# A graph-attention kernel on one core: ScalarE's part of the row loop traced one or two tiles later, counts and casts moved from VectorE to ScalarE

## The chip, the core and the metric

The kernel runs on one core of one Trainium2 chip. The metric is the device time of one execution in microseconds (us); lower is better. TensorE does the matrix products, VectorE, ScalarE and GpSimd do elementwise work, and SyncE issues most of the loads. Each engine runs its own instructions in order and waits for the others by semaphores. In the lines of the profile TensorE is PE (its weight loads PEld), VectorE DVE, ScalarE ACT, GpSimd POOL, SyncE SP.

## The reference

x has 3327 rows of 1024 numbers, adj is a symmetric 0/1 matrix of 3327 x 3327 with the diagonal set and about 17 ones in a row, and the weights are 1024 x 1024.

```python
h = maximum(layernorm(x), 0)
f = h @ Wf + bf
g = h @ Wg + bg
e = relu(f @ g.T)
scores = where(adj > 0, e, -9e15)
out = x + softmax(scores, axis=1) @ (h @ W + bW)
```

## The kernel before

The adjacency is sparse, so the kernel (`edge_path`) works on lists of neighbours. It has two parts. A dense fallback (`dense_path`) would run only if a list had not held its row's neighbours; with these inputs it does not.

**The first part** loops over 26 tiles `t` of 128 rows of x and adj (the last has 127). For each tile:

- `degrees(t)` loads the adjacency rows into `r`, of which there are four buffers. ScalarE turns them into floats in place with a Relu and sums them into the row's degree `deg` (L435). GpSimd multiplies by 1 + the column number (L436), so that `r` holds the numbers of the neighbours and zeros. The last two tiles do this in two halves.
- `normed(t)` makes h. It loads the rows of x into `xt` and finds mean and deviation: on VectorE for odd tiles (`bn_stats`, `bn_aggr` into `mv`, L406, L408; then ScalarE takes `nmr` and `rstd` from `mv`, L409, L410), on ScalarE for even ones (sum L414, L415, Square L417, Sqrt L418). VectorE takes the reciprocal (L419), ScalarE scales `nmr` (L420), computes the Relu of the normalized rows (L421) and issues the store to the table `hd` in memory (L423).
- `edges(t, r)` is VectorE's: in each of 16 segments of the row the 8 largest numbers (L446), 128 candidates `cand`; the count of positive ones (`cnt`, L448); then five times the 8 largest of the candidates into `lst` with a match_replace that takes these out (L452, L454), which gives the list of up to 40 neighbours; limits (L455), the cast into the payload `pay` (L456), the degree limited and cast (`dg`, L458, L459), and a one-hot of the degree `oh` (L460).
- `counted(t - 4)` counts, on TensorE with the result in `pre`, how many rows of each degree have come (L467, L472), and VectorE picks each row's rank out of it (`hit`, L469).
- `store_lists` writes the payload of four tiles to the table `pd`.

Beside this the loop prepares A = Wf Wg^T: in the first 8 tiles TensorE transposes row blocks of Wg, which ScalarE copies to `WgT` (L489, L490); in the next 8 iterations `make_A(c)` transposes a row block of Wf, multiplies (`ps_A`, L519, and `ps_u`, L525), and ScalarE copies the result (L522, L526). `make_rows` makes three rows from the biases (casts `terms`, L541).

After the loop VectorE and TensorE sort the rows by degree into `perm` (L575 to L612). `bads` collects what would call for the fallback.

**The second part** takes 128 rows at a time in the order of `perm`, gathers their lists and the h rows of their neighbours, and computes scores, softmax and output (L638 to L775). It takes most of the time and is not edited.

The order of instructions on each engine is set by a scheduler: it follows the order in which the program is traced as a priority and lets later instructions pass where it expects a wait. Each engine then runs its list strictly as compiled. A buffer is free again when the last reader of the tile before has finished.

Of the kernel before, what the change touches and what calls it, by code (L numbers as in the profile page):

```python
# [8 lines left out]
FP = mybir.dt.float32  # L9
I32 = mybir.dt.int32  # L10
AF = mybir.ActivationFunctionType
ALU = mybir.AluOpType
AX = mybir.AxisListType
# [6 lines left out]
BF = mybir.dt.bfloat16  # L20
SEG = 16
KM = 40
NBIN = 64
# [266 lines left out]
def edge_path(ctx: ExitStack, tc: tile.TileContext, x, adj, Wf, bf, Wg, bg, W, bW, out, flag):  # L290
# [10 lines left out]
    nc = tc.nc  # L301
    N, D = x.shape
    O = W.shape[1]
    P = 128
# [4 lines left out]
    NT = (N + P - 1) // P  # L309
# [4 lines left out]
    def rows(t):  # L314
        return min(P, N - t * P)
# [7 lines left out]
    const = ctx.enter_context(tc.tile_pool(name="const", bufs=1))  # L323
# [7 lines left out]
    eps = const.tile([P, 1], FP, name="eps")  # L331
# [2 lines left out]
    nc.gpsimd.iota(iotak, pattern=[[1, KM]], base=0, channel_multiplier=0, allow_small_or_imprecise_dtypes=True)  # L334
    ones3 = const.tile([3, P], BF, name="ones3")
    nc.gpsimd.memset(ones3, 1.0)
    bads = const.tile([P, NT + 2], FP, name="bads")
    nc.gpsimd.memset(bads, 0.0)


# [1 line left out]
    perm = const.tile([P, NT], I32, name="perm")  # L342
# [8 lines left out]
    with ExitStack() as part1:  # L351
        pool1 = lambda name, bufs, **kw: part1.enter_context(tc.tile_pool(name=name, bufs=bufs, **kw))
        c1 = pool1("c1", 1)
        wrow = pool1("wrow", 3)
        wT = pool1("wT", 2)
        ln = pool1("ln", 5)
        lnj = pool1("lnj", 1)
        kpool = pool1("key", 4)
        cpool = pool1("cand", 2)
        p_tr = pool1("p_tr", 2, space=PSUM)  # L360
        p_mm = pool1("p_mm", 2, space=PSUM)
        p_u = pool1("p_u", 1, space=PSUM)
# [29 lines left out]
        nc.gpsimd.memset(oh[:, NT - 1, :], 0.0)  # L392
        pre = p_c.tile([P, NBIN], FP, name="pre")

        def normed(t):

            n = rows(t)
            xt = ln.tile([P, D], FP, name="xt")
            for a, m in pieces(t):
                nc.sync.dma_start(xt[a : a + m], x[t * P + a : t * P + a + m, :])  # L400
            rstd = ln.tile([P, 1], FP, name="rstd")
            nmr = ln.tile([P, 1], FP, name="nmr")
            if t % 2:
                st = ln.tile([P, D // CB, 6], FP, name="st")
                for c in range(D // CB):
                    nc.vector.bn_stats(st[:n, c, :], xt[:n, c * CB : (c + 1) * CB])  # L406
                mv = ln.tile([P, 2], FP, name="mv")
                nc.vector.bn_aggr(mv[:n], st[:n])  # L408
                nc.scalar.activation(nmr[:n], mv[:n, 0:1], AF.Copy, scale=-1.0)  # L409
                nc.scalar.activation(rstd[:n], mv[:n, 1:2], AF.Sqrt, bias=eps[:n])  # L410
            else:
                sums = ln.tile([P, 2], FP, name="sums")
                j = lnj.tile([P, D], BF, name="lnj")
                nc.scalar.activation(j[:n], xt[:n], AF.Copy, accum_out=sums[:n, 0:1])  # L414
                nc.scalar.activation(nmr[:n], sums[:n, 0:1], AF.Copy, scale=-1.0 / D)  # L415
                j = lnj.tile([P, D], BF, name="lnj")
                nc.scalar.activation(j[:n], xt[:n], AF.Square, bias=nmr[:n], accum_out=sums[:n, 1:2])  # L417
                nc.scalar.activation(rstd[:n], sums[:n, 1:2], AF.Sqrt, bias=eps[:n], scale=1.0 / D)  # L418
            nc.vector.reciprocal(rstd[:n], rstd[:n])  # L419
            nc.scalar.activation(nmr[:n], nmr[:n], AF.Copy, scale=rstd[:n])  # L420
            nc.scalar.activation(xt[:n], xt[:n], AF.Relu, bias=nmr[:n], scale=rstd[:n])  # L421
            for a, m in pieces(t):
                nc.scalar.dma_start(hd[t * P + a : t * P + a + m, :], xt[a : a + m])  # L423

        def degrees(t):
            n = rows(t)
            r = kpool.tile([P, N], FP, name="r")
            a = r.bitcast(I32)
            for b, m in pieces(t):
                nc.sync.dma_start(a[b : b + m], adj[t * P + b : t * P + b + m, :])  # L430

            cuts = [0, SEG // 2 * SW, N] if t >= NT - 2 else [0, N]
            for i, (b, e) in enumerate(zip(cuts, cuts[1:])):
                to = deg[:n, t : t + 1] if not i else half[:n]
                nc.scalar.activation(r[:n, b:e], a[:n, b:e], AF.Relu, accum_out=to)  # L435
                nc.gpsimd.tensor_mul(r[:n, b:e], r[:n, b:e], iotaj[:n, b:e])  # L436
                if i:
                    nc.scalar.activation(deg[:n, t : t + 1], deg[:n, t : t + 1], AF.Identity, bias=half[:n])
            return r

        def edges(t, r):

            n = rows(t)
            cand = cpool.tile([P, SEG * 8], FP, name="cand")
            for s in range(SEG):
                nc.vector.max(cand[:n, s * 8 : s * 8 + 8], r[:n, s * SW : min(N, (s + 1) * SW)])  # L446
            pos = cpool.tile([P, SEG * 8], BF, name="pos")
            nc.vector.tensor_scalar(  # L448
                pos[:n], cand[:n], 0.0, None, op0=ALU.is_gt, op1=ALU.add, accum_out=cnt[:n, t : t + 1]
            )  # L450
            for i in range(0, KM, 8):
                nc.vector.max(lst[:n, i : i + 8], cand[:n])  # L452
                if i + 8 < KM:
                    nc.vector.match_replace(cand[:n], lst[:n, i : i + 8], cand[:n], 0.0)  # L454
            nc.vector.tensor_scalar(lst[:n], lst[:n], float(N), 1.0, op0=ALU.min, op1=ALU.max)  # L455
            nc.vector.tensor_scalar(pay[:n, t, :KM], lst[:n], -1.0, None, op0=ALU.add)  # L456
            dg = cpool.tile([P, 1], FP, name="dg")
            nc.vector.tensor_scalar(dg[:n], deg[:n, t : t + 1], float(NBIN - 1), None, op0=ALU.min)  # L458
            nc.vector.tensor_copy(pay[:n, t, KM : KM + 1], dg[:n])  # L459
            nc.vector.tensor_scalar(oh[:n, t, :], iotad[:n], dg[:n], None, op0=ALU.is_equal)  # L460

        def counted(t):

            n = rows(t)


            nc.tensor.matmul(pre, tri, oh[:, t, :], start=(t == 0), stop=False, skip_group_check=True)  # L467
            hit = cpool.tile([P, NBIN], FP, name="hit")
            nc.vector.scalar_tensor_tensor(  # L469
                hit[:n], pre[:n], 1.0, oh[:n, t, :], op0=ALU.mult, op1=ALU.mult, accum_out=rp[:n, t : t + 1]  # L470
            )
            nc.tensor.matmul(pre, low, oh[:, t, :], start=False, stop=(t == NT - 1), skip_group_check=True)  # L472
# [60 lines left out]
        def make_rows():  # L533

            ps = p_u.tile([P, P], FP, name="ps_u")
            for k in range(KD):
                nc.tensor.matmul(ps[0:1, 0:1], bfT[:, k : k + 1], bgT[:, k : k + 1], start=(k == 0), stop=(k == KD - 1))
            nc.scalar.copy(cols[:, :KD], v_ps)
            nc.scalar.copy(cols[0:1, 2 * KD :], ps[0:1, 0:1])
            for i in range(3):  # L540
                nc.vector.tensor_copy(terms[:, i, :], cols)  # L541
                if i < 2:
                    nc.vector.tensor_sub(cols, cols, terms[:, i, :])
            for row, first in ((v3, 0), (bW3, KD)):
                for o in range(OH):
                    ps = p_mm.tile([P, CB], FP, name="ps_A")
                    for k in range(CB // P):
                        c = first + o * (CB // P) + k
                        nc.tensor.matmul(ps[:3, k * P : (k + 1) * P], terms[:, :, c], identb, start=True, stop=True)
                    nc.scalar.copy(row[:, o * CB : (o + 1) * CB], ps[:3])  # L550
            ps = p_u.tile([P, P], FP, name="ps_u")
            nc.tensor.matmul(ps[:3, 0:1], terms[:, :, 2 * KD], identb[:, 0:1], start=True, stop=True)
            nc.scalar.copy(v3[:, D : D + 1], ps[:3, 0:1])

        for t in range(NT):
            r = degrees(t)
            normed(t)
            edges(t, r)
            if t >= LAG:
                counted(t - LAG)  # L560
            if t % 4 == 3 and t > 4:
                store_lists(t - 7, t - 3)
            if t < KD:
                load_Wg(t)
            elif t < 2 * KD:
                make_A(t - KD)
            if t == 2 * KD:
                make_rows()
        for t in range(NT - LAG, NT):
            counted(t)  # L570
        store_lists(20, NT)
# [34 lines left out]
            )  # L606
        tens = c1.tile([P, NT], FP, name="tens")
        nc.vector.tensor_copy(tens, ps[:, NT : 2 * NT])
        nc.vector.scalar_tensor_tensor(perm, ps[:, :NT], float(P), tens, op0=ALU.mult, op1=ALU.add)
        over = c1.tile([P, 1], FP, name="over")  # L610
        nc.vector.tensor_scalar(over, part, float(rows(NT - 1)), float(N), op0=ALU.is_ge, op1=ALU.mult)
        nc.vector.tensor_tensor(final, perm[:, NT - 1 : NT], over, op=ALU.add)  # L612
# [2 lines left out]
        nc.vector.tensor_reduce(bads[:, NT : NT + 1], ne, AX.X, ALU.max)  # L615
        nc.vector.tensor_scalar(ne, deg, 1.0, None, op0=ALU.is_lt)
        nc.vector.tensor_reduce(bads[:, NT + 1 : NT + 2], ne, AX.X, ALU.max)


    W_sb = ctx.enter_context(tc.tile_pool(name="W", bufs=1)).tile([P, KD, O], FP, name="W_sb")  # L620
# [239 lines left out]
```

## Time and profile before

| | us |
|---|---|
| median of 14 runs | 1463.4 |
| lowest and highest of them | 1441.2, 1489.4 |
| profiled execution, own time | 1469.4 |
| its span, first to last instruction | 1467.7 |
| tile loop of the first part, until the last multiply on GpSimd ends | 263.7 |
| `perm` ready, second part begins | 284 |

| Engine | busy in the whole span | share |
|---|---|---|
| VectorE | 1221.4 us | 83% |
| TensorE | 1179.9 us | 80% |
| GpSimd | 875.0 us | 60% |
| ScalarE | 474.7 us | 32% |

The shares are means over two parts with different limits: ScalarE, with 32% over the whole, is busy for 69% of the time from tile 2 to tile 24 in the first part. So what an edit of the first part is worth must be read from that stretch alone. A line of the timeline has its start, its duration, the engine, the line of the kernel, the operation, result and inputs with their shapes, and in brackets how long the engine had been idle and what ended that. A line of the list of waits has who waited for whom, then the total, the number of waits and the longest.

### The profile page before, as it was taken

To read this page: it belongs to the slowest core of one execution; us is meant where nothing else is said; L and a number is where in the kernel's file an instruction comes from. 1 tells how busy PE (TensorE), PEld (TensorE's weight loads), DVE (VectorE), ACT (ScalarE), POOL (GpSimd) and SP (SyncE) were. 2 spreads that over 40 slices of the span, in tenths; PEclk is the share of its full clock that TensorE was granted. 3 is DMA by queue.
4 is the path that set the end of the run, shared out by engine and by line. 5 is a ranking of instruction groups with operands and counts; after the bars stand their busy time and mean duration, and the time that the engine had idled before them with its cause. 6 is when DMAs were issued, how large, how long until landed. Compare 5 with 4: busy or idle time off the path is not lost.

```text
span 1467.7 us, 14137 instructions
## 1 busy us (share of the span) xinstructions
PE 1179.9 (80%) x4355; PEld 685.5 (47%) x4355; DVE 1221.4 (83%) x2550; ACT 474.7 (32%) x738; POOL 875.0 (60%) x628
## 2 busy tenths in 40 slices
PE   4579996057188798999779878899889998999784
PEld 4445453034065455555345444555445554555331
DVE  4888889609979889898887789898899989999980
ACT  6666767101063144433122321222222222121110
POOL 8677776262656466666464456666667676666501
PEclk9999998579599899999889888999999999999887
DMA  9897895392678798887695677777878878788812
GB/s 369 334 346 315 309 324 170 113 407 65 235 243 294 243 329 281 306 284 229 241 320 171 232 262 268 260 231 245 263 245 290 281 234 257 259 274 276 256 30 59
DMA packets 97710, 372.52 MB, mean 254 GB/s; under 512 B 14268, under 2 KB 14684, under 8 KB 94297
## 3 DMA queue, kind: packets, MB, share of 16 engines
q0 software_dynamic: 79552, 286.85, 58.3%
q1 hardware_dynamic: 10860, 70.49, 12.5%
q10 hardware_dynamic: 7212, 14.18, 2.8%
q8 instruction: 36, 0.59, 0.2%
q14 instruction: 50, 0.41, 0.1%
HBM read 343.67 MB, written 27.80 MB: 253 GB/s over the span
## 4 chain that ended last, share of the span: by engine, by line
PE 27%; issue 26%; POOL 17%; DVE 15%; DMA 5%; ACT 5%; another core or an unknown queue 4%; POOLq 0%; ACTq 0%; SPq 0%; DVEq 0%
PE ps_o L759 13%; POOL r L436 9%; PE ps_q L667 8%; DVE y L747 6%; POOL G L638 6%; DMA G<-hd,pi 4%; PE yT_ps L725 3%; DVE junk L684 3%; DVE cand L446 2%; ACT G L741 2%; PE ps_A L519 1%; DMA res<-in_x_dram,perm 1%; POOL res L638 1%; DVE sc L684 1%
## 5 line engine op out<-in xcount | busy, mean ns | idle before, releaser
L638 POOL DMA_INDIRECT G<-hd,pi x468 | 545.4, 1165 | 276.5 <-issue 111.3
L684 DVE CUSTOM_DVE_ANT_0 junk<-G,q 128x1024 bf16<-128x1024 f32 x468 | 601.3, 1285 | 87.2 <-DMA G<-hd,pi 49.3
L667 PE MATMUL ps_q<-A_sb,hT 128*128 128x342 f32 x1248 | 395.4, 465 | 76.5 <-ACT q L669 46.0
L759 PE MATMUL ps_o<-W_sb,yT 128*128 128x512 f32 x832 | 394.6, 630 | 33.9 <-ACT yT L754 19.6
L747 DVE SCALAR_TENSOR_TENSOR y<-G,sc,y 128x1024 f32<-128x1024 f32 x320 | 412.0, 1288 | 11.2 <-ACT y L745 9.4
L667 PEld LDWEIGHTS ps_q<-A_sb,hT 128*128 128x128 f32 x1248 | 231.6, 193 | 195.0 <-ACT q L669 47.0
L759 PEld LDWEIGHTS ps_o<-W_sb,yT 128*128 128x128 f32 x832 | 163.8, 202 | 238.5 <-issue 212.8
L436 POOL TENSOR_TENSOR r<-r,iotaj 128x3327 f32<-128x3327 f32 (+4 forms) x28 | 188.6, 6743 | 66.0 <-ACT r L435 50.7
L446 DVE MAX8 cand<-r 128x8 f32<-128x208 f32 (+2 forms) x416 | 136.3, 372 | 34.7 <-POOL r L436 34.7
L741 ACT ACTIVATE G<-G,sc 128x1024 f32<-128x1024 f32 x122 | 129.8, 1137 | 0.0
L519 PE MATMUL ps_A<-WgT,WfT 128*128 128x512 f32 x256 | 119.7, 628 | 3.0 <-ACT WfT L490 3.0
L761 ACT COPY res<-ps_o 128x512 f32<-128x512 f32 x52 | 30.4, 585 | 280.2 <-PE ps_o L760 248.7
L725 PE MATMUL yT_ps<-ident,G 128*128 128x128 f32 x976 | 116.6, 275 | 2.0 <-ACT G L741 1.4
L725 PEld LDWEIGHTS yT_ps<-ident,G 128*128 128x128 f32 x976 | 107.0, 140 | 15.1 <-issue 5.8
L669 ACT COPY q<-ps_q 128x342 f32<-128x342 f32 x78 | 33.5, 450 | 218.0 <-PE ps_q L668 87.3
L638 POOL DMA_INDIRECT res<-in_x_dram,perm x26 | 45.5, 1751 | 83.2 <-ACT res L761 80.2
L754 ACT COPY yT<-yT_ps 128x512 f32<-128x512 f32 x52 | 27.9, 588 | 194.8 <-issue 80.6
L519 PEld LDWEIGHTS ps_A<-WgT,WfT 128*128 128x128 f32 x256 | 50.9, 202 | 66.3 <-issue 62.1
L725 PE MATMUL yT_ps<-ident,y 128*128 128x128 f32 x208 | 35.4, 324 | 55.1 <-DVE y L747 25.3
L435 ACT ACTIVATE r<-r 128x3327 f32<-128x3327 int32 (+4 forms) x28 | 77.5, 2767 | 0.1
L767 POOL DMA_INDIRECT out_dram<-res,perm x25 | 28.2, 1129 | 73.2 <-DMA res<-in_x_dram,perm 73.2
L651 ACT COPY hT<-ps_t 128x512 f32<-128x512 f32 x52 | 29.7, 592 | 114.0 <-PE ps_q L667 71.1
(139 smaller groups left out, 790.1 us busy)
## 6 DMA issues: line engine op xcount, KB each, us to landing
r<-in_adj_dram SPq DMA_DIRECT2D x25, 1663.5 KB, 9.0
xt<-in_x_dram SPq DMA_DIRECT2D x25, 512.0 KB, 11.5
hd<-xt ACTq DMA_DIRECT2D x25, 512.0 KB, 6.0
G<-hd,pi POOLq DMA_INDIRECT x468
wr<-in_L_gnn_Wg_dram SPq DMA_DIRECT2D x8, 512.0 KB, 11.9
wr<-in_L_gnn_Wf_dram SPq DMA_DIRECT2D x8, 512.0 KB, 7.6
W_sb<-in_L_gnn_W_dram SPq DMA_DIRECT2D x1, 4096.0 KB
r<-in_adj_dram SPq DMA_DIRECT2D x1, 1455.6 KB, 8.8
```

The costliest lines, as they stand in the source:

```text
L435: nc.scalar.activation(r[:n, b:e], a[:n, b:e], AF.Relu, accum_out=to)
L436: nc.gpsimd.tensor_mul(r[:n, b:e], r[:n, b:e], iotaj[:n, b:e])
L446: nc.vector.max(cand[:n, s * 8 : s * 8 + 8], r[:n, s * SW : min(N, (s + 1) * SW)])
L519: nc.tensor.matmul(ps, WfT[:, k, :], WgT[:, k, o * CB : (o + 1) * CB], start=(k == 0), stop=(k == KD - 1))
L638: nc.gpsimd.indirect_dma_start(out=to, out_offset=None, in_=table, in_offset=bass.IndirectOffsetOnAxis(ap=idx, axis=0), **kw,)
L667: nc.tensor.matmul(ps[:, :QB], hT[:, k, :], A_sb[:, k, o : o + QB], start=(k == 0), stop=False)
L669: nc.scalar.copy(q[:, o : o + QB], ps[:, :QB])
L684: nc.vector.tensor_tensor_reduce(junk, g, e["q"][:, :D], 1.0, e["q"][:, D : D + 1], op0=ALU.mult, op1=ALU.add, accum_out=e["sc"][:, k : k ...
L725: nc.tensor.matmul(e["yT"][:, c, :], g[:, c * P : (c + 1) * P], ident, is_transpose=True, start=(first and c % 4 == 0), stop=(last and c % ...
L741: nc.scalar.activation(g, g, AF.Copy, scale=p)
L747: nc.vector.scalar_tensor_tensor(y, g, p, y, op0=ALU.mult, op1=ALU.add)
L759: nc.tensor.matmul(ps, yT[:, k, :], W_sb[:, k, o * CB : (o + 1) * CB], start=(k == 0), stop=False)
```

## The change

Four things change in the first part.

1. `normed(t)` is cut in three. It keeps the load, the statistics, and for even tiles the mean and the Sqrt. `scaled(t)` has `nmr` and `rstd` of odd tiles, and the reciprocal; `stored(t)` has the scaling of `nmr`, the Relu of h and its store. They are traced in the next iteration: `scaled(t - 1)` at its start, `stored(t - 1)` after `normed(t)`.
2. The count of the candidates, the cast of the list and the cast of the degree move from VectorE to ScalarE, as `kept(t)`, traced two iterations later. The count is now the sum of signs.
3. VectorE's list steps write to `rest` instead of over `cand`, so that `cand` stays for the count; the limited list goes to `ids` in SBUF. The degree is no longer limited to 63; instead a third test in `bads` asks whether a degree is 64 or more, and `perm` is limited to the last row by one operation more.
4. `ln` gets six buffers instead of five and `cand` four instead of two; `hit` and the count's other output go to a pool with one buffer.

```diff
-        ln = pool1("ln", 5)
+        ln = pool1("ln", 6)
-        cpool = pool1("cand", 2)
+        cpool = pool1("cand", 4)
...
         def normed(t):
...
+            lns[t] = xt, rstd, nmr
             if t % 2:
...
                 nc.vector.bn_aggr(mv[:n], st[:n])
-                nc.scalar.activation(nmr[:n], mv[:n, 0:1], AF.Copy, scale=-1.0)
-                nc.scalar.activation(rstd[:n], mv[:n, 1:2], AF.Sqrt, bias=eps[:n])
+                lns[t] += (mv,)
             else:
...
+        def scaled(t):
+            n = rows(t)
+            xt, rstd, nmr, *mv = lns[t]
+            if mv:
+                nc.scalar.activation(nmr[:n], mv[0][:n, 0:1], AF.Copy, scale=-1.0)
+                nc.scalar.activation(rstd[:n], mv[0][:n, 1:2], AF.Sqrt, bias=eps[:n])
             nc.vector.reciprocal(rstd[:n], rstd[:n])
+
+        def stored(t):
+            n = rows(t)
+            xt, rstd, nmr, *mv = lns.pop(t)
             nc.scalar.activation(nmr[:n], nmr[:n], AF.Copy, scale=rstd[:n])
             nc.scalar.activation(xt[:n], xt[:n], AF.Relu, bias=nmr[:n], scale=rstd[:n])
...
         def edges(t, r):
...
-            pos = cpool.tile([P, SEG * 8], BF, name="pos")
-            nc.vector.tensor_scalar(
-                pos[:n], cand[:n], 0.0, None, op0=ALU.is_gt, op1=ALU.add, accum_out=cnt[:n, t : t + 1]
-            )
+            rest = lnj.tile([P, SEG * 8], FP, name="rest")
+            of = cand
             for i in range(0, KM, 8):
-                nc.vector.max(lst[:n, i : i + 8], cand[:n])
+                nc.vector.max(lst[:n, i : i + 8], of[:n])
                 if i + 8 < KM:
-                    nc.vector.match_replace(cand[:n], lst[:n, i : i + 8], cand[:n], 0.0)
-            nc.vector.tensor_scalar(lst[:n], lst[:n], float(N), 1.0, op0=ALU.min, op1=ALU.max)
-            nc.vector.tensor_scalar(pay[:n, t, :KM], lst[:n], -1.0, None, op0=ALU.add)
-            dg = cpool.tile([P, 1], FP, name="dg")
-            nc.vector.tensor_scalar(dg[:n], deg[:n, t : t + 1], float(NBIN - 1), None, op0=ALU.min)
-            nc.vector.tensor_copy(pay[:n, t, KM : KM + 1], dg[:n])
-            nc.vector.tensor_scalar(oh[:n, t, :], iotad[:n], dg[:n], None, op0=ALU.is_equal)
+                    nc.vector.match_replace(rest[:n], lst[:n, i : i + 8], of[:n], 0.0)
+                    of = rest
+            ids = cpool.tile([P, KM], FP, name="ids")
+            nc.vector.tensor_scalar(ids[:n], lst[:n], float(N), 1.0, op0=ALU.min, op1=ALU.max)
+            found[t] = cand, ids
+            nc.vector.tensor_scalar(oh[:n, t, :], iotad[:n], deg[:n, t : t + 1], None, op0=ALU.is_equal)
+
+        def kept(t):
+            n = rows(t)
+            cand, ids = found.pop(t)
+            pos = lnj.tile([P, SEG * 8], BF, name="pos")
+            nc.scalar.activation(pos[:n], cand[:n], AF.Sign, accum_out=cnt[:n, t : t + 1])
+            nc.scalar.activation(pay[:n, t, :KM], ids[:n], AF.Copy, bias=-1.0)
+            nc.scalar.copy(pay[:n, t, KM : KM + 1], deg[:n, t : t + 1])
...
         for t in range(NT):
+            if t:
+                scaled(t - 1)
             r = degrees(t)
             normed(t)
+            if t:
+                stored(t - 1)
+            if t >= 2:
+                kept(t - 2)
             edges(t, r)
...
+        scaled(NT - 1)
+        stored(NT - 1)
+        kept(NT - 2)
+        kept(NT - 1)
         for t in range(NT - LAG, NT):
             counted(t)
...
-        nc.vector.scalar_tensor_tensor(perm, ps[:, :NT], float(P), tens, op0=ALU.mult, op1=ALU.add)
+        place_of = c1.tile([P, NT], FP, name="place_of")
+        nc.vector.scalar_tensor_tensor(place_of, ps[:, :NT], float(P), tens, op0=ALU.mult, op1=ALU.add)
+        nc.vector.tensor_scalar(perm, place_of, float(N - 1), None, op0=ALU.min)
...
+        nc.vector.tensor_scalar(ne, deg, float(NBIN), None, op0=ALU.is_ge)
+        nc.vector.tensor_reduce(bads[:, NT + 2 : NT + 3], ne, AX.X, ALU.max)
```

More of the change, by code (lines that the diff above doesn't have):

```diff
@@ L336, in edge_path @@
     nc.gpsimd.memset(ones3, 1.0)
-    bads = const.tile([P, NT + 2], FP, name="bads")
+    bads = const.tile([P, NT + 3], FP, name="bads")
     nc.gpsimd.memset(bads, 0.0)
@@ L393, in edge_path @@
         pre = p_c.tile([P, NBIN], FP, name="pre")
+        lns = {}
         def normed(t):
@@ L439, in degrees @@
             return r
+        found = {}
         def edges(t, r):
@@ L467, in counted @@
             nc.tensor.matmul(pre, tri, oh[:, t, :], start=(t == 0), stop=False, skip_group_check=True)
-            hit = cpool.tile([P, NBIN], FP, name="hit")
+            hit = lnj.tile([P, NBIN], FP, name="hit")
             nc.vector.scalar_tensor_tensor(
```

## The prediction

> **What bounds the kernel now.** The change lies in the first part, so I read the busy table by stretches first. GpSimd's multiply by the column numbers (L436) starts tile 2 at 29.68 us, tile 8 at 88.98, tile 16 at 166.83 and tile 24 at 240.88; I cut there.
>
> ```profile
> 29.68:88.98 59.30, 32.92 (x153) 30.66 (x153) 49.96 (x252) 40.35 (x61) 43.44 (x7) 1.00 0.93 362
> 88.98:166.83 77.85, 70.32 (x225) 36.19 (x224) 65.84 (x323) 53.44 (x83) 57.93 (x8) 0.98 0.79 304
> 166.83:240.88 74.05, 69.08 (x230) 35.73 (x229) 64.07 (x318) 53.11 (x84) 58.06 (x9) 0.95 0.87 307
> ```
>
> The columns are length, PE, PEld, DVE, ACT, POOL, TensorE clock, DMA share. Two tiles take 19.8, 19.5 and 18.5 us, but GpSimd works only 14.5 of them. VectorE is busy 86% and nobody is full. So waits set the pace; the list of waits (30 to 240 us) says whose:
>
> ```profile
> POOL r L436 <- ACT r L435: 41.1, 14, 6.0
> DVE cand L446 <- POOL r L436: 30.5, 12, 3.7
> ACT nmr L420 <- DVE rstd L419: 23.8, 9, 4.9
> ACT A_sb L522 <- PE ps_A L519: 15.2, 6, 4.3
> ACT nmr L409 <- DVE mv L408: 10.6, 4, 3.5
> ACT nmr L409 <- DVE dg L458: 9.4, 4, 3.5
> ```
>
> GpSimd waits for ScalarE's Relu of the adjacency rows (L435), VectorE for GpSimd, ScalarE for VectorE: a ring. The timeline shows one turn:
>
> ```profile
> 77.20 0.38 DVE L446 MAX8 cand<-r 128x8 f32<-128x208 f32 x1 [3.31 <-POOL r L436]
> 80.82 0.29 ACT L420 ACTIVATE nmr<-nmr,rstd 128x1 f32<-128x1 f32 x1 [3.29 <-DVE rstd L419]
> ...
> 85.55 0.20 ACT L409 ACTIVATE nmr<-mv 128x1 f32<-128x1 f32 x1 [2.35 <-DVE dg L458]
> 85.85 2.96 ACT L435 ACTIVATE r<-r 128x3327 f32<-128x3327 int32 x1
> 88.98 7.25 POOL L436 TENSOR_TENSOR r<-r,iotaj 128x3327 f32<-128x3327 f32 x1 [4.15 <-ACT r L435]
> ...
> 96.66 7.24 POOL L436 TENSOR_TENSOR r<-r,iotaj 128x3327 f32<-128x3327 f32 x1 [0.44 <-DVE cand L446]
> ```
>
> GpSimd ends tile 6 at 77.17; VectorE's maxima, mixed with the previous tile's list, and tile 7's statistics take until 85.5; only then can ScalarE start tile 8's Relu (85.85), GpSimd 3.13 us later. Every second multiply starts late, the next at once. From tile 9 a second ring joins: a row block of A on TensorE (L519, L525, then the transposes L489), whose copies stand in ScalarE's queue.
>
> ```profile
> 170.40 15.67 PE L519 MATMUL ps_A<-WgT,WfT 128*128 128x512 f32 x32
> ...
> 189.41 14.00 PE L519 MATMUL ps_A<-WgT,WfT 128*128 128x512 f32 x32 [0.67 <-ACT WfT L490]
> 203.25 1.84 PE L525 MATMUL ps_u<-bgT,WfT 128*128 128x1 f32 x16
> 204.96 1.07 PE L489 MATMUL ps_tr<-ident,wr 128*128 128x128 f32 x8
> ```
>
> From a block's start to its last transpose 16.5 us, 18.1 where the clock was cut, plus the copies.
>
> **What the Trainium skill says.** "Perfetto Trace Analysis", section "Tensor Engine Instruction", calls ScalarE, VectorE and GpSimd strict FIFO. The trace agrees: ScalarE idles 3.29 us at L420 with a Relu behind it. "SBUF — State Buffer", section "Who interferes with whom", says that a VectorE cast or tensor_scalar with source and result in SBUF may enter a two-port mode that excludes GpSimd for a whole instruction. The trace agrees: the 17-column cast L541 takes 0.17 us at 245.66 and 3.54 at 246.87, GpSimd multiplying from 246.69 to 250.37. The new ids operation reads PSUM, so it should stay as short as L456 (192 ns).
>
> **The change part by part.** I read the instruction order of the changed program as compiled; the second part's order is the same on every engine, so its cost is 0, and it shifts with perm.
>
> *VectorE loses* per tile L448 (291 + 97 ns), L456 (192), dg L458 (149) and its cast L459 (158): 0.89 us of busy time, 23 us in 26 tiles. These overlap their neighbours; start to start (149.84 to 150.14 for two of them) about 0.55 us, 14 us in all. But the list operations now mostly follow each other instead of lying between maxima: one max and one match_replace then take 0.73 us (151.22 to 151.95) instead of 0.45. Four such pairs cost 1.1 us, so VectorE gains nothing net. I work it out at 16 maxima 4.42, list 3.5, statistics 0.7, one hit and the rest 0.6: about 9.2 us a tile. It fits the rings below, with little slack.
>
> *ScalarE gains* three instructions a tile. No row shows Sign on 128 columns; nearest are 199 ns (1 column, L415) and 1047 (1024, L414), so 0.31 with an accumulator read of which 0.09 shows. The order has no further table load. Bounds 0.25 and 0.6 us; I take 0.31. The cast of ids 0.14, that of the degree 0.10. 0.55 us a tile, 14 us in all; ScalarE has 30% idle, but these stand in the ring.
>
> *The waits move.* ScalarE's order is now, for even B: Relu(B); sum over B; nmr scaling (B-1), which waits for reciprocal(B-1); counts and casts (B-2); Square(B); Relu of h(B-1) and its store; copies; Relu(B+1). VectorE has reciprocal(B-1) after all 16 maxima of B-1. So a wait goes (mv ahead of the Relu) and another comes: GpSimd's end of B-1 -> maxima -> reciprocal -> ScalarE's queue -> Relu(B+1) -> GpSimd B+1. Behind it are queued Square, h's store, the TensorE copies and the Relu.
>
> One turn, two tiles, while WgT is built: maxima 4.42 (20.60 to 25.02) + reciprocal until seen 0.23; ScalarE scaling 0.2, mean 0.1, Sign 0.31, Square 1.14, Relu of h 1.13, Sqrt 0.2, store issue 0.3, casts 0.24, two copies 0.95 = 4.57; Relu to GpSimd 3.14; GpSimd 7.25. Sum **19.6 us**, against 19.8 now: tiles 2 to 8, 3 turns, -0.5 us.
>
> Tiles 8 to 14: two A copies join (+0.65): 20.2 against 19.95 measured (88.98 to 148.82): +0.8 us.
>
> Tiles 14 to 24: the order puts the copies before the scaling, where they hide behind the maxima: 18.65. But TensorE needs the hit of an earlier tile, which VectorE does after an odd tile's reciprocal, before it starts the next block. Where that decides, two turns are 1.1 + 16.45 to 18.15 (block) + copies and sum 2.0 + 3.6 + 3.14 + 7.25 + 4.65 = 38.2 to 39.9, or 19.1 to 19.95 each. It decides in about half the turns; I take 19.2 against 18.4 measured (148.82 to 240.88): 5 turns, +4.0 us.
>
> *End of part 1.* Tile 25's Relu waits behind the copies of v and bW, these for the casts L541; now the first of the three meets the second half of tile 24's multiply, before it was the third: +1 (bounds 0 and +3.7). After the last multiply VectorE is spared tile 25's four operations, -0.9; perm needs one more of 0.22. Sum +0.3. The third failure test (two operations of 0.17) lies between list steps.
>
> *SP and DMA.* No DMA is added. x and adj loads are issued a little otherwise; adj has four buffers, and the wait from a buffer's release to its Relu is over 20 us against 9.0 us of landing, so 0; were that cover gone, 9 us once per late load. h's store, one tile later, lands some 10 us before perm: 0. The extra buffers of ln and cand cost nothing.
>
> Sum: -0.5 + 0.8 + 4.0 + 0.3 = **+4.6 us**. The profiled execution took 1469.4 us (span 1467.7 and 1.7 around it), 6.0 above the median; it would take 1474.0, and the median goes from 1463.4 to **1468**.
>
> **The rivals.**
> *VectorE's load is the limit* (faster). 86% busy and the many short waits speak for it. If every saved step counts, 14 us (start to start) to 23 us (busy) go: 1440 to 1449. Against it: the 30.5 us that VectorE waits for GpSimd, and the order, in which the reciprocal still stands behind 16 maxima. If all of GpSimd's 41.1 us of waiting went: 1422, a bound; VectorE's 9.2 us a tile forbid it.
> *TensorE's ring decides every turn* (slower). The hit after an odd tile's reciprocal starts each block; with the clock cut as at 170 us, 19.95 per turn in tiles 14 to 24 is +7.7 instead of +4.0; with the cast's upper bound and a late first block (the Wf copies wait for tile 7's reciprocal: 3 us later than now, by the turns above) up to +14: 1471 to 1478. It decides once a block's end plus copies comes after the odd tile's reciprocal, that is from a block over 16 us. For it: the 14.0 us block already is there. Against: ScalarE waits for it only 15.2 us.
> *The move is undone by the scheduler*: no; the order shows it.
>
> **How the numbers follow.** A difference of 0.5% (7.3 us) is about what a measurement can tell. My ring sums, 0.3 us each over 11 turns, are good to some 5 us around +4.6, so about half lies within 7.3. No change to measure, most likely a little up: 0.46. Slower by more (TensorE's ring): 0.38. Faster by more (VectorE's load): 0.16. Range 1448 to 1482: it holds the likeliest case (1460 to 1473), the slower one and the mild end of the faster.
>
> **What would show it.** Right: GpSimd still waits for Relu before every second multiply, now the odd tiles, 4 to 5 us; tile 8 starts within 2 us of 88.98, tile 24 3 to 8 us after 240.88; ScalarE's longest wait on VectorE is nmr <- rstd, and that on mv is gone; list steps at 0.73 us. Wrong: multiplies back to back, or tile 24 before 235 us; or a second part of other length than now.

## The result, and the profile after

The changed kernel's median is 1466.95 us (10 runs, 1457.7 to 1488.4), that of the kernel before 1465.5 (47 runs, 1436.2 to 1492.1). The ratio is 1.012 (95% interval 1.0075 to 1.0164); it leaves out every run over 1.5% above the fastest of its own kernel, which keeps most runs of the changed kernel (mean 1467.2 us) but only the 16 fastest of the other's 47 (mean 1449.7), so that most of these 17 us comes from the choice of runs. The medians lie 1.5 us apart, and single runs of one program scatter by 2% here, more than the effect. A repeat on a chip where they scatter by some 0.6% to either side gave 1424.9 us (22 runs) against 1418.4 (30 runs), **1.0041 (1.0023 to 1.0058)**, or +6.5 us (again_after_2 below).

The stretches of the changed kernel, cut at the start of GpSimd's multiply of tiles 2, 8, 16 and 24 (length, then busy PE, PEld, DVE, ACT, POOL, TensorE clock, DMA share, GB/s):

```profile
29.89:88.75 58.86, 31.03 (x144) 28.55 (x144) 50.81 (x226) 43.83 (x83) 43.46 (x7) 1.00 0.94 359
88.75:166.36 77.61, 71.29 (x224) 37.39 (x225) 66.42 (x280) 59.09 (x114) 58.01 (x9) 0.98 0.88 332
166.36:244.56 78.20, 70.20 (x239) 37.11 (x238) 66.71 (x284) 58.77 (x117) 58.01 (x9) 0.93 0.80 274
```

Before they took 59.30, 77.85 and 74.05 us: the loss lies in the last stretch, +4.15. ScalarE (the sixth figure) works 5.7 us longer in each of the last two. VectorE has a tenth fewer instructions, but is at least as busy as before.

The list of waits, 30 to 240 us (who waited for whom: total, times, longest):

```profile
POOL r L450 <- ACT r L449: 51.4, 17, 4.3
PE pre L490 <- DVE oh L473: 25.8, 8, 5.0
ACT nmr L434 <- DVE rstd L428: 24.0, 16, 4.2
DVE cand L462 <- POOL r L450: 22.8, 18, 2.4
PE pre L495 <- DVE hit L492: 13.3, 10, 3.4
ACT A_sb L545 <- PE ps_A L542: 13.1, 9, 4.1
```

GpSimd waits 10 us longer for ScalarE's Relu of the adjacency rows, VectorE 8 us less for GpSimd; the wait on mv is gone, that on the reciprocal (rstd) is as long and comes 16 times instead of 9. And the end of the first part, GpSimd's timeline:

```profile
244.56 3.71 POOL L450 TENSOR_TENSOR r<-r,iotaj 128x1664 f32<-128x1664 f32 x1 [0.49 <-ACT r L449]
249.78 3.72 POOL L450 TENSOR_TENSOR r<-r,iotaj 128x1663 f32<-128x1663 f32 x1 [1.51 <-ACT cols L562]
261.34 7.36 POOL L450 TENSOR_TENSOR r<-r,iotaj 127x1664 f32<-127x1664 f32 x2 [7.85 <-DVE rest L468]
```

7.85 us of waiting stand before tile 25, against 5.95 in the profile before. The second part's first gather is issued at 288.9 us, 4.0 later than before (284.9), and what follows takes 1180.4 us against 1182.8. In these two executions the first part lost 4.0 us and the second nothing.

### The profile page after: what moved, and what is told of

It is laid out like the page before. It is cut to its first block, busy times and chain, and to the rows that moved or that the text cites. A ratio compares the mean times of both kernels' runs of the same rounds, so it can differ in the third digit from the quotient of the medians.

```text
span 1469.3 us, 14105 instructions
## 1 busy us (share of the span) xinstructions
PE 1184.5 (81%) x4355; PEld 689.3 (47%) x4355; DVE 1224.5 (83%) x2423; ACT 490.4 (33%) x842; POOL 874.4 (60%) x628
## 4 chain that ended last, share of the span: by engine, by line
PE 27%; issue 21%; DVE 14%; DMA 6%; another core or an unknown queue 5%; POOL 5%; ACT 2%; POOLq 0%; ACTq 0%; DVEq 0%
PE ps_o L798 14%; DVE y L786 8%; PE ps_q L706 7%; PE yT_ps L764 5%; POOL G L677 4%; DMA G<-hd,pi 4%; DVE junk L723 4%; DMA pi<-pd,perm 1%; DVE sc L723 1%; ACT hT L690 1%; PE ps_o L799 1%; DMA hp<-hd,perm 1%; DMA res<-in_x_dram,perm 0%; ACT q L708 0%
## 5 line engine op out<-in xcount | busy, mean ns | idle before, releaser
L462 DVE MAX8 cand<-r 128x8 f32<-128x208 f32 (+2 forms) x416 | 123.6, 368 | 31.0 <-POOL r L450 31.0
L764 PE MATMUL yT_ps<-ident,G 128*128 128x128 f32 x976 | 118.8, 277 | 10.2 <-ACT G L780 7.3
L449 ACT ACTIVATE r<-r 128x3327 f32<-128x3327 int32 (+4 forms) x28 | 77.6, 2773 | 0.0
```

Source lines behind the costliest of these rows:

```text
L764: nc.tensor.matmul(e["yT"][:, c, :], g[:, c * P : (c + 1) * P], ident, is_transpose=True, start=(first and c % 4 == 0), stop=(last and c % ...
```

## Experiments

**1. Change or scatter?** Theory 1: the change costs 4 to 5 us, in the first part alone; the rest of the 1.012 is scatter. Theory 2: the second part is slower too. Theory 3: the first part costs 12 to 17 us in most runs. Both kernels were run again, and both with the second part cut away:

```diff
-    prepare(0)
-    prepare(1)
-    for i, (s, k0, k1) in enumerate(units):
...
+    r0 = xpool.tile([P, O], FP, name="res")
+    gather(r0, hd[:, :], perm[:, 0:1])
+    nc.sync.dma_start(out[:P, :], r0)
+    bad = failed()
```

> The kernel before, unchanged, timed as if it were another kernel. Theory 1 (the change costs 4 to 5 us in the first part, and the rest of the measured ratio of 1.012 is the scatter of single runs, +-2% for one and the same program, met by 10 runs of one kernel and 47 of the other): a median within 10 us of 1465, and a ratio that may stray from 1 by up to 1% though nothing differs. Theory 2 (the second part of the changed kernel is really some 12 us slower): a ratio of 1.000 within 0.3%, that is, a comparison that strays much less than 1.2%.

> The changed kernel, once more. Theory 1: median 1460 to 1475, that is +2 to +8 us against the copy of the kernel before in the same call, and the second part (from its first gather to the end) within the scatter of the copy's own, 1165 to 1200 us. Theory 2: a ratio of 1.010 to 1.015 again, +15 to +21 us against the copy, and a second part longer by 10 us or more than the copy's.

> The kernel before with its second part left out: after the order of the rows is known it gathers one block of h by it and stores that. The end of the first part was at 284.9 us in the profile of the whole kernel; one gather and one store after it: 293 to 303 us, with a scatter of well under 1%, as there are no list-driven gathers left. Both theories expect this; if single runs scatter by 2% here too, the scatter is not of the second part.

> The changed kernel with its second part left out in the same way. Theory 1 and theory 2: +3.5 to +5.5 us against the first part of the kernel before (the profiles of the whole kernels gave +4.0). Theory 3 (the profiled execution was a lucky one, and the first part itself costs 12 to 17 us in most runs): +12 us or more.

> The changed kernel once more, on whatever chip this is. Theory 1 (first part +8, the rest is scatter): +3 to +10 us against before, ratio 1.002 to 1.007. Theory 2 (second part slower as well): +15 us or more, 1.010 to 1.015.

Measured: on one chip 1460.5 us for the copy of before (6 runs, 1428.9 to 1467.8), 1457.6 for the changed kernel (6 runs), 1463.3 for before itself (12 runs): no difference to see in that scatter. The first parts alone: 302.8 us (301.4 to 307.3) before, **311.0** (309.2 to 311.7) after. That is +8.2, not the expected 4, and far from 12 to 17. The 5.8 us of scatter before are 2%, where well under 1% was expected. On the quiet chip the whole kernel: +6.5 us. So theory 1 holds in kind: the loss is the first part's. Of its size half was missing.

**2. The other half: one cast's luck.** In the copy of before the last multiply starts at 252.65 us, in the first part alone at 256.41, though tile 24 starts within 0.3 us in both. VectorE's timeline, first of the copy, where GpSimd's half multiply starts at 246.64:

```profile
246.54 0.18 DVE L541 CAST terms<-cols 128x17 bf16<-128x17 f32 x1
```

then of the first part alone, where it starts at 246.77:

```profile
246.95 3.54 DVE L541 CAST terms<-cols 128x17 bf16<-128x17 f32 x1
250.40 0.29 DVE L452 MAX8 held<-cand 128x8 f32<-128x128 f32 x1
```

and of the changed first part, where it starts at 250.20:

```profile
250.19 0.18 DVE L564 CAST terms<-cols 128x17 bf16<-128x17 f32 x1 [0.49 <-ACT cols L562]
250.27 0.30 DVE L466 MAX8 held<-rest 128x8 f32<-128x128 f32 x1
250.47 3.48 DVE L566 TENSOR_TENSOR cols<-cols,terms 128x17 f32<-128x17 f32 x1
```

The cast that started 0.10 us ahead of the multiply escaped; the one that started 0.18 us after it waited for the multiply's end. After the change the first cast escapes by 0.01 us, and the subtraction behind it is held instead; so it was in all four profiles of the changed kernel with the rows in this place (tile 25 at 261.2 to 261.8). The Trainium skill's page "SBUF — State Buffer", section "Who interferes with whom", says both: a cast in a two-port mode excludes GpSimd, and a tensor_tensor with two SBUF inputs contends with GpSimd's reads. The runs agree, 0.16 to 0.18 us free against 3.48 to 3.54 held. In the kernel before this is a toss (held in two of three profiles, though 5 of the 6 runs of its first part were at least 2.8 us shorter than the one whose profile shows it); in the changed kernel it was lost in every profile. There the hold reaches ScalarE, whose copies of the rows stand ahead of tile 25's Relu (p1_after):

```profile
255.70 1.05 ACT L573 CAST v<-ps_A 3x512 bf16<-3x512 f32 x2 [2.90 <-PE ps_A L572]
```

The test: make the rows v and bW, whose casts these are, after the last tile.

```diff
-            if t == 2 * KD:
-                make_rows()
...
         store_lists(20, NT)
+        make_rows()
```

> First part only of the kernel before, with the rows v and bW made after the last tile (make_rows called after the last lists are stored) and not beside tile 24. Theory 1 (before loses 3.7 us of the tail in those runs in which the third 17-column cast falls into GpSimd's half multiply of 3.7 us, and none in the others): 300 to 302 us in every run, within 1.5 us of each other, against 301.4 to 307.3 of p1_before; the cast takes under 0.3 us. Theory 2 (the scatter of p1_before is the clock or the transfers): the same scatter of 4 to 6 us.

> First part only of the changed kernel, with the rows v and bW made after the last tile. Theory 1 (of the 8 us that p1_after is longer than the usual p1_before, 4 are lost by tile 24 and 4 by the cast or subtraction that always meets the multiply): 303.5 to 306 us, 3 to 5 us over p1_before_rows. Theory 2 (all 8 us are lost in the turns of ScalarE, wherever the rows are made): 307 to 311 us, 6 to 9 us over p1_before_rows.

Measured: 303.0 us (302.4 to 304.2) and 304.0 (302.2 to 306.2). The changed kernel gains 7.0 us, of which GpSimd's timeline shows 5.5 before tile 25 (256.30 us instead of 261.77); before gains nothing, since its tail after tile 25 grows. The difference shrinks from 8.2 to 1.0 us, though tile 24 is still 3.3 us late (244.71 against 241.43). The scatter of p1_before_rows is 1.8 us instead of 5.8, which is theory 1's way, but its 300 to 302 us and its 3 to 5 us between the two were missed; the scatter of p1_after_rows, 4 us in four runs, was not explained. The test also takes the rows' own copies, some 2 us, out of ScalarE's queue before tile 25, so its 5.5 us are not the hold alone.

The two copies of the whole kernels give the account: tile 24 starts at 241.12 and 244.93 us (+3.8), tile 25 at 252.65 and 261.73 (+9.1), the first gather is issued at 281.2 and 289.3 (+8.1). Of the 5.3 us between the tiles, 4.0 are the toss (from tile 24 to 25 before takes 11.5 us with luck, 15.6 without); the rest was not taken apart.

**3. Which half of the change costs until tile 24?** The two halves alone (both keep the pools of part 4 of the change and the third test in `bads`, so the share of these is not known):

```diff
 (p1_delay: edges() as before, no kept())
-            if t >= 2:
-                kept(t - 2)
 (p1_moved: scaling and storing where they were)
-            if t:
-                scaled(t - 1)
             r = degrees(t)
             normed(t)
-            if t:
-                stored(t - 1)
+            scaled(t)
+            stored(t)
```

> First part only (second part left out, as in p1_before), with the first half of the change alone: scaling and storing of h traced a tile later; counts and casts stay on VectorE. Theory 1 (the new place of the scaling costs, as it puts ScalarE's wait for the odd tile's reciprocal ahead of the next Relu of adjacency rows and TensorE's next block behind the odd tile's hit): GpSimd starts tile 24 at 243 to 246 us, as in the changed kernel (244.97), against 240.9 of before. Theory 2 (the counts and casts in ScalarE's queue and the list steps that now follow each other on VectorE cost): tile 24 within 1 us of 240.9.

> First part only, with the second half of the change alone: counts and casts on ScalarE two tiles later; scaling and storing where they were before. Theory 1: tile 24 within 1.5 us of 240.9, or up to 3 us earlier, as VectorE is spared 0.55 us a tile. Theory 2: tile 24 at 243 to 246 us, and list steps 0.73 us a pair.

Both theories fell. The first half alone is *faster*: tile 24 at 237.6 us, p1_delay 302.6 in all (its tail gives the gain back). The second half alone is 18 us slower: tile 24 at 258.8, 321.3 in all. Together they lose 3.5. The stretches of all kernels, from their timelines (us):

| kernel | tiles 2 to 8 | 8 to 16 | 16 to 24 | sum | to before |
|---|---|---|---|---|---|
| before | 59.3 | 77.9 | 74.1 | 211.2 | |
| changed | 58.9 | 77.6 | 78.2 | 214.7 | +3.5 |
| p1_delay | 58.3 | 76.4 | 73.4 | 208.1 | -3.1 |
| p1_moved | 71.9 | 80.1 | 77.3 | 229.3 | +18.1 |
| p1_dup | 59.5 | 81.7 | 80.1 | 221.4 | +10.2 |
| p1_drop | 57.2 | 79.5 | 75.3 | 212.0 | +0.8 |
| p1_mixed | 60.7 | 80.4 | 80.1 | 221.1 | +9.9 |
| p1_placed | 59.0 | 82.0 | 79.8 | 220.8 | +9.6 |
| p1_short | 59.1 | 77.1 | 77.4 | 213.6 | +2.4 |
| p1_after_quarter | 58.9 | 84.3 | 79.9 | 223.1 | +11.9 |

**4. What about the move costs?** Two kernels take its sides apart. p1_dup leaves counts and casts on VectorE and makes them again on ScalarE; p1_drop makes them nowhere. p1_mixed holds VectorE's list steps between the maxima of the next tile by ordering edges:

```diff
 (p1_dup: p1_delay, and)
+            if t >= 2:
+                again(t - 2)      # as kept(), into tiles nobody reads; the list's cast reads a constant tile
             edges(t, r)
 (p1_drop: the changed kernel)
-            nc.scalar.activation(pos[:n], cand[:n], AF.Sign, accum_out=cnt[:n, t : t + 1])
-            nc.scalar.activation(pay[:n, t, :KM], ids[:n], AF.Copy, bias=-1.0)
-            nc.scalar.copy(pay[:n, t, KM : KM + 1], deg[:n, t : t + 1])
 (p1_mixed: the changed kernel)
+                with tc.issue_after(step.ins) if step else nullcontext():
+                    biggest = nc.vector.max(...)
+                with tc.issue_after(biggest.ins):
+                    step = next(listing[0], None)
```

> First part only. The first half of the change (delay), counts and casts stay on VectorE, and ScalarE makes them a second time, two tiles later, into tiles that nobody reads: the ScalarE side of the move without the VectorE side. p1_delay starts tile 24 at 237.6 us, the changed kernel at 244.97. Theory A (the move costs because VectorE's list steps then follow each other: in the instruction order of the changed kernel 56 of 104 match_replace stand directly between two list maxima, 5 before, none with the delay alone, and 22 here): tile 24 at 238.5 to 241 us. Theory B (the three instructions in ScalarE's queue cost, VectorE's order doesn't): 243 to 246 us.

> First part only, of the changed kernel with counts and casts made nowhere (left out, cnt and the lists filled with constants): the VectorE side of the move without the ScalarE side. 28 of 104 match_replace stand between two list maxima. Theory A: tile 24 at 239 to 243 us, in spite of less work on both engines than p1_delay (237.6). Theory B: 234 to 237 us.

> First part only, of the changed kernel, with the list steps of tile t-1 held one by one between the maxima of tile t on VectorE by ordering edges (1 of 104 match_replace between two list maxima; same instructions as p1_after). Theory A: tile 24 at 234 to 239 us against 244.97 of p1_after. Theory B: 243 to 246 us, no gain. Theory C (the reciprocal sets the pace, and list steps ahead of it delay it by 2.5 us a tile): 246 us or later.

Measured: tile 24 of p1_dup starts at 252.7 us, beyond both theories; counted from tile 2 that is +13.3 us against p1_delay, for three instructions of 0.55 us a tile, 12 us in 22 tiles (ScalarE's busy time grew by 9.3). So here they cost what they take or more, and theory A (the list steps' order) did not account for it. p1_mixed, with the lists hardly ever in a row, is 6.5 us slower than the changed kernel, as theory C said: theory A does not hold in this form. But the edges also put each list and its one-hot `oh` a tile later, so p1_mixed tests more than the order. (p1_drop's and p1_short's totals, 4032 and 4037 us, contain the fallback that runs when counts disagree; only the first part is read.) p1_drop starts tile 24 at 241.45 us, 3.8 us later than p1_delay, with less work on both engines: theory B expected 234 to 237, so ScalarE's three instructions cannot be the whole cost of the move. The four kernels don't add up: ScalarE's operations cost 13.3 us with VectorE's in place and 2.7 us (changed less p1_drop) without. The scheduler orders each kernel anew; the timelines don't say how much of this is its order. They do show what p1_drop waits for. The same line of the list of waits (30 to 240 us), of p1_delay and of p1_drop:

```profile
ACT A_sb L536 <- PE ps_A L533: 9.3, 6, 2.6
ACT A_sb L542 <- PE ps_A L539: 22.5, 10, 5.4
```

ScalarE waits 13 us longer for TensorE's blocks of A, and p1_drop loses only where there are blocks: to tile 8 it is 1.0 us faster than p1_delay.

The stretches of p1_delay and of p1_dup (same columns as above), from tile 2 on:

```profile
29.49:87.75 58.26, 32.00 (x148) 29.31 (x148) 50.61 (x255) 41.36 (x61) 43.44 (x6) 1.00 0.94 365
87.75:164.19 76.44, 72.00 (x241) 38.54 (x241) 66.29 (x318) 55.36 (x84) 58.07 (x8) 0.96 0.83 319
164.19:237.61 73.42, 68.71 (x227) 35.44 (x227) 64.78 (x325) 54.07 (x85) 58.04 (x8) 0.95 0.89 310
```

```profile
31.33:90.85 59.52, 32.68 (x150) 29.59 (x150) 51.10 (x257) 43.59 (x80) 43.42 (x6) 1.00 0.93 334
90.85:172.59 81.74, 70.05 (x218) 36.05 (x218) 67.37 (x317) 57.94 (x109) 57.97 (x8) 0.98 0.82 311
172.59:252.72 80.13, 71.88 (x238) 37.72 (x237) 70.26 (x327) 58.60 (x117) 57.91 (x9) 0.91 0.82 279
```

From tile 2 to 8, ahead of A's copies, 2.2 us more on ScalarE cost 1.3 us. With A's copies in its queue, 2.6 and 4.5 us more cost 5.3 and 6.7. My reading, not tested alone: a copy that is late holds up TensorE's next block as well as the next Relu.

**5. The place of the odd Relu.** p1_delay's ScalarE, in one turn (ScalarE's timeline):

```profile
186.50 0.29 ACT L434 ACTIVATE nmr<-nmr,rstd 128x1 f32<-128x1 f32 x1 [0.49 <-DVE rstd L428]
186.70 0.19 ACT L417 ACTIVATE nmr<-sums 128x1 f32<-128x1 f32 x1
186.80 2.96 ACT L449 ACTIVATE r<-r 128x3327 f32<-128x3327 int32 x1
```

and the changed kernel's:

```profile
189.57 0.29 ACT L434 ACTIVATE nmr<-nmr,rstd 128x1 f32<-128x1 f32 x1 [1.57 <-DVE rstd L428]
189.78 0.19 ACT L417 ACTIVATE nmr<-sums 128x1 f32<-128x1 f32 x1
189.87 0.29 ACT L481 ACTIVATE pos<-cand 128x128 bf16<-128x128 f32 x1
...
190.16 1.14 ACT L419 ACTIVATE lnj<-xt,nmr 128x1024 bf16<-128x1024 f32 x1
...
191.29 1.23 ACT L435 ACTIVATE xt<-xt,nmr,rstd 128x1024 f32<-128x1024 f32 x1
...
193.26 2.98 ACT L449 ACTIVATE r<-r 128x3327 f32<-128x3327 int32 x1
```

With the delay alone the odd Relu comes 0.3 us after the scaling; in the changed kernel the Sign stands in that place, and the Relu comes 3.7 us after it. Is that the cost? p1_placed traces Square, the Relu of h, counts and casts after the odd Relu, and gets p1_delay's order back between the scaling and that Relu:

```diff
...
             r = degrees(t)
+            if (t - 1) in squares:
+                squared(t - 1)
+                if t >= 2:
+                    stored(t - 2)
+                if t >= 3:
+                    kept(t - 3)
+                scaled(t - 1)
             normed(t)
...
```

> First part only, of the changed kernel, with the Square and the Relu of h of two tiles, and the counts and casts, traced after the odd tile's Relu of adjacency rows. ScalarE's order of p1_delay from one Relu to the other comes back (odd Relu right after mean, scaling and sum of the even tile), with the six moved instructions of two tiles behind it. Theory D (the move costs because the Sign operation takes the place on ScalarE in which the planner had put the odd Relu, so that this Relu stands behind Square, Relu of h, Sqrt and casts): tile 24 at 234 to 240 us against 244.97 of p1_after. Theory B (three more instructions a tile cost wherever they stand): 243 to 252 us.

> First part only: p1_placed with the rows v and bW made after the last tile. Theory D: 296 to 300 us, at most the 298.2 of p1_delay_rows, as VectorE is spared 0.55 us a tile besides. Theory B: 303 us or more.

Theory D fell: tile 24 at 251.0 us, 314.6 in all, and 311.2 with the rows last. The odd Relu is early, and the even one pays: from 197.21 to 208.98 us ScalarE idles 2.8 us, and both tiles' counts and casts lie between the two Relus, which start 11.8 us apart instead of p1_delay's 10.6 (186.80 to 197.41). Wherever they stand in the turn, they stand ahead of one of the two. That is one turn, and not the only thing p1_placed changed: its ScalarE waits 28.9 us for A's blocks (30 to 240 us) instead of p1_delay's 9.3.

**6. Size, and TensorE's ring.** p1_short makes the Sign on 8 columns; p1_after_quarter takes 2 of the 8 terms of A.

```diff
-            nc.scalar.activation(pos[:n], cand[:n], AF.Sign, accum_out=cnt[:n, t : t + 1])
+            nc.scalar.activation(pos[:n, :8], cand[:n, :8], AF.Sign, accum_out=cnt[:n, t : t + 1])
 (p1_after_quarter)
-                for k in range(KD):
+                for k in range(2):
...
```

> First part only, of the changed kernel, with the Sign operation on 8 of the 128 columns (the counts leave the rest out), so some 0.1 us less on ScalarE a tile and nothing else; ScalarE's order from tile 8 on is that of p1_after but for one tile. Theory B (in the ring each turn of two tiles carries both tiles' operations of ScalarE, so that 24 tiles pay in full): 1.5 to 3 us off tile 24, at 241.5 to 243.3 us against 244.4 to 245.0 in the runs of the changed kernel. Rival (ScalarE's operations lie beside VectorE's wait, one set a turn or none counts): 243.8 to 245 us.

> First part only, of the changed kernel, with the product A made from 2 of its 8 terms (a quarter of TensorE's matmuls for it left out of no other thing: copies, transposes, rows stay, and are done earlier). If TensorE's ring decides about half of the turns after tile 10, as predicted, tiles 10 to 18 take 72 to 74 us against 76.0 in the changed kernel (108.9 to 184.9). If the ring of ScalarE, GpSimd and VectorE decides them, 75 to 77 us there, and only the tiles after the last copy of A get faster, by ScalarE's 1 us of copies a turn.

p1_short: the Sign went from 296 to 192 ns, 2.3 us over 22 tiles. Tile 24 starts at 242.9 us, where theory B had it and 1.5 to 2.1 us before the changed kernel's runs; counted from tile 2, 1.1 to 1.8. It points to B but does not carry it alone. p1_after_quarter missed both theories (89.7 us from tile 10 to 18): from tile 8 to 16 it is 6.7 us *slower* than the changed kernel, with TensorE less busy, at a granted clock of 0.84 instead of 0.98 (same columns):

```profile
88.66:172.96 84.30, 64.95 (x265) 39.74 (x265) 70.63 (x293) 66.45 (x134) 58.02 (x9) 0.84 0.87 316
```

A's blocks, now short, follow faster, so more of their copies come in these turns: ScalarE is busy 66.45 us instead of 59.09, and the stretch grows by about as much. TensorE had slack here (77% busy instead of 92%; from 30 to 240 us it waits 62.6 us for oh instead of 25.8), so its ring is not what made these turns long; ScalarE's own work fits. (In the stretch after it, one wait of 9.94 us stands before tile 18, where the rows are now made.)

In the changed kernel itself TensorE's ring does end some turns. Its timeline, VectorE and ScalarE:

```profile
197.98 0.16 DVE L428 RECIPROCAL rstd<-rstd 128x1 f32<-128x1 f32 x1
...
200.40 0.59 ACT L545 COPY A_sb<-ps_A 128x512 f32<-128x512 f32 x1 [4.07 <-PE ps_A L542]
200.89 0.30 ACT L434 ACTIVATE nmr<-nmr,rstd 128x1 f32<-128x1 f32 x1
```

The scaling, behind which the next Relu is queued, does not wait for the reciprocal, done at 198.14 us, but for the block's copy ahead of it, which starts 2.3 us later. This happens in three turns (copies at 159.82, 200.40 and 239.41 us; 3.4 us in all). The two other profiles of the whole changed kernel and that of p1_after have three such turns each, the three profiles with the delay alone have none. So of what the move costs, a part goes through TensorE's blocks; no run tested that part alone.

**7. A version faster than both.** The delay alone, with the rows made last:

> First part only: the first half of the change (delay) with the rows v and bW made after the last tile. If the two gains add (3.3 us by tile 24, and a tail free of the cast that meets GpSimd's multiply): 298 to 300.5 us against 302.6 of p1_delay and 303.0 of p1_before_rows. If the tail takes the gain back, as it did in p1_delay: 302 to 303.5 us.

> The whole kernel with the first half of the change alone and the rows v and bW made after the last tile. Its first part took 298.2 us alone, against 302.8 of before: 3 to 6 us less than before, a ratio of 0.996 to 0.998, which a comparison may not tell from 1. If the second part starts from another state and loses it: 1.000.

p1_delay_rows took 298.2 us (297.6 to 298.9), 4.6 less than before's first part. The whole kernel took 1411.75 us (9 runs) against 1418.4 (30 runs, same chip): **0.9947 (0.9923 to 0.9971)**, or 6.6 us less, a little more than expected. Its first gather is issued at 276.5 us.

## Why the prediction was wrong, and what in it held

The forecast was no change to measure: +4.6 us, 1468 us as the median. The median of the first comparison, 1466.95, met that number, in a scatter that hides the effect. The repeat on the quiet chip shows that the change costs time: +6.5 us, with an interval that leaves 1 out. That is within the 5 us that the forecast allowed its sum, but two of its steps failed: the cause of the loss in the turns, where two errors happened to cancel, and the size of the end of the first part.

- *The second part only shifts*: right, 1180.4 us after and 1182.8 before.
- *VectorE gains nothing net*: right. Busy 50.81, 66.42 and 66.71 us in the three stretches, against 49.96, 65.84 and 64.07. Where the list steps follow each other they take 0.73 us a pair (p1_after: 238.25, 238.98, 239.71), and the wait moved from mv to rstd as said. GpSimd's wait of some 4 us before the odd tiles came from tile 13 on (3.98 to 4.27); before that every tile waits, 1.5 to 3.5 us.
- *What bounds the kernel*: nobody was called full, while the lines shown there have TensorE busy 69.08 of 74.05 us (93%) in the last stretch.
- *The turns*: the sum to tile 24 was +4.3 by its terms; measured +3.5, and tile 24 at +3.7 us. Term by term, at the cuts of the prediction (tile 14 starts at 148.82 us before, 146.07 in the changed kernel, 145.32 in p1_delay, 143.94 in p1_drop; differences to before in us):

| | tiles 2 to 8 | 8 to 14 | 14 to 24 | sum |
|---|---|---|---|---|
| forecast | -0.5 | +0.8 | +4.0 | +4.3 |
| changed | -0.4 | -2.5 | +6.4 | +3.5 |
| p1_delay | -1.0 | -2.3 | +0.2 | -3.1 |
| p1_drop | -2.1 | -2.6 | +5.5 | +0.8 |

- *Why the turns lose*: the first step that failed. It gave the loss to the delay, by a new ring over the reciprocal and TensorE's blocks. The delay alone gains 3.1 us, and +0.2 came of its +4.0 after tile 14; the move costs 6.6 on top, 6.2 of them after tile 14. Of these 6.2 us p1_drop has 5.2 without one of the three ScalarE instructions. What the step says of the blocks is seen in the changed kernel (three turns, 3.4 us), but the move brought it, not the delay. The other side was too small in the sum of a turn: I counted one Sign and one pair of casts, and a turn of two tiles carries two sets; in p1_dup they cost 13.3 us. That the sum was met is luck: the delay's gain of 3.1 us and the move's cost of 6.6, neither of which stands in it, come to about the same.
- *The end of the first part, +0.3*: the second step that failed, a term that was mis-sized. Against the one execution it was worked out from it holds: +3.7 at tile 24, +4.0 at the first gather. But it took that execution's 3.54 us cast as what the kernel before always pays, and most runs of its first part do not pay it. Against those the term is +4.3 (from +3.8 at tile 24 to +8.1). The bounds of 0 and +3.7 were put on the changed kernel's cast alone, none on before's; and the subtraction between the casts, the one that is held, was left out.
- *The rivals*: VectorE's load as the limit did not come (p1_drop). TensorE's ring deciding every turn gave 1471 to 1478; +6.5 to +8.2 us on 1463.4 would be 1470 to 1472, about its lower end. A block ended last in three of the five turns after tile 14, not in every one, and half of the loss is the tail's.

Open: how the move's 6.6 us divide between ScalarE's instructions, TensorE's blocks and the new orders, and why the move costs 18 us without the delay. Orders of instructions differ between all these kernels on VectorE and ScalarE, and no run kept one order while it changed one duration (p1_short came nearest).

## What to carry to other kernels

A short instruction that may or may not collide with a long one is a coin toss: here 0.10 us ahead was free and 0.18 us behind cost 3.5 us. Look for such pairs in the profile, price both sides, and compare several executions before calling one of them the kernel. When work is moved off the busiest engine in a ring to an engine that the ring also passes, count every set that a turn carries on the receiving engine: 0.55 us a tile on ScalarE, idle 30% of the time, cost 13 us in 22 tiles in one pair of kernels and 2.7 in another, so price it with a run and not with the sum alone. And try the halves of a change alone: here one half won, the other lost, and together they looked like nothing.

## What the runs showed of the hardware

The kernel before took 1417 to 1419 us (medians) on three chips and 1456 and 1463 on two others, where single runs also scatter more. The first part does not show it: tile 24 of p1_delay_rows starts at 237.60 us on one of the latter, that of full_delay_rows at 238.19 on one of the former. The second part of the changed kernel took 1180.4 us in its first profile and 1137.5 in again_after_2's. A subtraction of 17 columns on VectorE (two SBUF inputs) was held 3.48 us by a GpSimd multiply, just as the cast was.
